# Attention logits in 32x64 tiles of TensorE: two column tiles of 64 keys for each head in place of one of 128

## The chip, the cores and the metric

The kernel runs on one core of a Trainium2 chip. The metric is the device time of one execution in microseconds (us); the median of three executions stands for the kernel.

## What is computed

The input x has the shape 4 x 128 x 64 x 64 (images, channels, rows, columns). Layer 0 normalises over the channels, adds a 3x3 depthwise convolution, and computes neighbourhood attention inside windows of 16x16 pixels: 2 branches, 4 heads of 32 channels, every pixel looks at the 5x5 pixels around it. Layer 1 treats the 4096 pixels of an image as tokens: causal linear attention, then a normalised recurrence over the tokens. The part that the change touches is this, for each window, branch b and head h:

```
k_nb = _patches(k, KSZ)
v_nb = _patches(v, KSZ)
scale = HD ** (-0.5)
logits = jnp.einsum('nbhdij,nbhdkij->nbhkij', q, k_nb) * scale
attn = jax.nn.softmax(logits, axis=3)
o = jnp.einsum('nbhkij,nbhdkij->nbhdij', attn, v_nb)
```

Here n is the window, d runs over the 32 channels of a head, k over the 25 neighbours and ij over the 256 pixels.

## The kernel before

**Staging.** The image is cut into 16 bands (4 images x 4 bands of 16 rows), each band into 4 windows of 16x16 pixels: 64 windows in all. For every band the kernel normalises and convolves (`norm_rows`, `convolve`, the taps on VectorE are L288), and for every window it goes through three steps that overlap between windows. `window_inputs` (L330) makes q, k (L337 on TensorE, evicted at L345) and v (L350, L357). `logits` (L370) makes the masked logits of both branches and their exponentials. `weighted` (L394) makes the denominators (L400), the weighted values (L412), and sends the denominators through DMA to be inverted on VectorE (L423 to L427) and spread again (L429, L431). `scaled` (L440, GpSimd) multiplies both. `layer1` (L608) is the linear attention of a band, written as a fixed order of steps; it runs two bands' halves in the gaps of later windows: among its lines are the output projection L465, transposes L212 by way of `turned`, queries and keys L494 (with L496 on ScalarE, L498 and L499 on VectorE), values L511 and L519, key transposes L529, scores L537 and L539, states L554 and L562, outputs L573, L575 and L587, and the product L602 with L603 and L604. After the last window comes a recurrence (L822, L835) and the output.

**The logits.** For a window, the four heads lie on partitions 0-31, 32-63, 64-95 and 96-127 of q and k, which are [128, 512]: branch times 256 pixels. Keys are handled in blocks of 8 rows of 16 pixels, so 128 keys; queries come in three pieces for each branch, rows 0 to 5, 6 to 9 and 10 to 15 (96, 64 and 96 pixels), each with the block of keys that holds all their neighbours: `BLOCKS`. Head h has a PSUM bank of its own, `sps[h]`: 128 keys on the partitions, 512 queries along the bank. First comes the mask (L377): a product of bfloat16 one-hot keys with query rows of 0 and -1e30, over all 512 queries. The six pieces are then accumulated onto it in float32 (L382), and four exponentials read the banks (L391). The stationary operand is the block of keys, [32 rows x 128 columns], the moving operand the queries, [32 x 96 or 64]. Four heads therefore use four row tiles of 32x128 in the array. A float32 matmul call appears in the trace as two weight loads and two matmuls, a bfloat16 call as one of each: per window 4 + 48 matmuls for the logits. The weighted values (L412) are the mirror image: the stationary operand is [128 keys x 32 channels], in four column tiles of 128x32, the moving operand has the same 96, 64 and 96 queries.

**The order of the work.** [...] `in_order` (L160) fixes that order for TensorE, VectorE, ScalarE and GpSimd. In the loop at L699, turn i issues `logits` of window i, `scaled` of window i-2, `weighted` of window i-1 and `window_inputs` of window i+1. Between these, six calls of `between` each take one step of `layer1` (`behind`) and one of normalisation and convolution (`ahead`). A window is called by its place wj = 0 to 3 in the band below; the layer-1 work of a band starts in the window with wj = 1 of the next band. All PSUM tiles of this part come from one pool of eight banks, used in rotation (L176), so the four banks of the logits must be free before the masks start.

## Time and profile before

| what | value |
|---|---|
| median of three executions | 929.56 us (928.55 to 930.22) |
| span of the profiled execution | 933.3 us |
| the 64 windows: first and last start of L382 | 26.2 and 803.8 us |
| TensorE matmuls busy | 878.8 us, 94% of the span |
| TensorE weight loads busy | 657.1 us, 70% |
| VectorE busy | 734.2 us, 79% |
| ScalarE busy | 539.5 us, 58% |
| GpSimd busy | 257.5 us, 28% |
| mean granted TensorE clock | 0.977 of full speed |

The page gives no other time for the profiled execution than its span, which is 3.7 us longer than the median. The timeline lists instructions in order of time, neighbours of one kind merged: start, duration, engine, line, operation, operands, and in brackets the idle time of the engine just before and who ended it. PE is the matmul side of TensorE, PEld its weight loads, DVE is VectorE, ACT ScalarE, POOL GpSimd. A matmul's recorded duration holds its latency too, so matmuls overlap, and a PE that shows no idle time may still stand for a fraction of a microsecond. In the steady state, 110 to 760 us, a band of four windows takes about 50.5 us; the four windows from L377 at 402.37 us on, for example, start at 402.37 (wj = 3), 413.57 (wj = 0), 427.82 (wj = 1) and 441.23 (wj = 2).

### The profile page before, as it was taken

To read this page: it belongs to the slowest core of one execution; us is meant where nothing else is said; L and a number is where in the kernel's file an instruction comes from. 1 tells how busy PE (TensorE), PEld (TensorE's weight loads), DVE (VectorE), ACT (ScalarE), POOL (GpSimd) and SP (SyncE) were. 2 spreads that over 40 slices of the span, in tenths; PEclk is the share of its full clock that TensorE was granted. 3 is DMA by queue.
4 is the path that set the end of the run, shared out by engine and by line. 5 is a ranking of instruction groups with operands and counts; after the bars stand their busy time and mean duration, and the time that the engine had idled before them with its cause. 6 is when DMAs were issued, how large, how long until landed. Compare 5 with 4: busy or idle time off the path is not lost.

```text
span 933.3 us, 26460 instructions
## 1 busy us (share of the span) xinstructions
PE 878.8 (94%) x10508; PEld 657.1 (70%) x10508; DVE 734.2 (79%) x2408; ACT 539.5 (58%) x1010; POOL 257.5 (28%) x358
## 2 busy tenths in 40 slices
PE   4968999999999999999999999999999999977894
PEld 3846787777787777778777777777777778755452
DVE  6454888889797879798888889787878787577694
ACT  3654656575656565665657575656666565522553
POOL 2112141323222232314132323323231403131174
PEclk9988999999999999999999999999999999989898
DMA  4111112122212121211212121212121111111853
GB/s 121 25 46 57 42 51 58 56 59 63 59 48 61 48 66 49 73 38 57 55 54 60 59 60 48 62 51 65 48 71 37 60 36 56 36 35 32 351 223 143
DMA packets 53045, 63.46 MB, mean 68 GB/s; under 512 B 22960, under 2 KB 33840, under 8 KB 52400
## 3 DMA queue, kind: packets, MB, share of 16 engines
q1 hardware_dynamic: 51184, 56.91, 19.6%
q10 hardware_dynamic: 1728, 4.77, 1.3%
q8 instruction: 85, 1.39, 0.7%
q14 instruction: 48, 0.39, 0.1%
HBM read 35.44 MB, written 17.30 MB: 57 GB/s over the span
## 4 chain that ended last, share of the span: by engine, by line
PE 59%; DVE 25%; DMA 5%; ACT 3%; issue 3%; POOL 3%; ACTq 0%; SPq 0%; DVEq 0%; POOLq 0%
DVE y L288 9%; PE bank L337 9%; PE bank L465 7%; PE bank L382 6%; PE bank L212 6%; PE bank L494 5%; PE bank L400 4%; PE bank L350 4%; PE bank L412 3%; PE bank L602 3%; DMA res<-resd 2%; DVE st L191 2%; PE bank L537 2%; DVE state L562 2%; DVE x L587 2%
## 5 line engine op out<-in xcount | busy, mean ns | idle before, releaser
L288 DVE SCALAR_TENSOR_TENSOR y<-ypad,cpe_w,y 128x512 f32<-128x512 f32 x240 | 191.5, 798 | 17.4 <-ACT y L286 13.9
L391 ACT ACTIVATE es<-bank 128x512 f32<-128x512 f32 x256 | 132.2, 603 | 77.3 <-PE bank L382 77.3
L440 POOL TENSOR_TENSOR oT<-o_sb,rden 128x512 f32<-128x512 f32 x64 | 83.9, 1311 | 247.3 <-DMA rden<-rd 221.5
L195 POOL TENSOR_SCALAR rs<-mv 128x4 f32<-128x4 f32 (+2 forms) x100 | 25.0, 250 | 366.1 <-DVE mv L193 162.8
L203 DVE TENSOR_SCALAR xn<-x,mv,rs 128x128 f32<-128x128 f32 x256 | 89.5, 411 | 26.5 <-POOL rs L196 26.5
L196 POOL TENSOR_TENSOR rs<-rs,mhalf 128x4 f32<-128x4 f32 (+2 forms) x100 | 106.3, 1063 | 8.3
L382 PEld LDWEIGHTS bank<-q,k 32*128 32x128 f32 x3072 | 97.8, 189 | 9.7 <-ACT k L345 8.5
L382 PE MATMUL bank<-q,k 32*128 32x96 f32 (+1 forms) x3072 | 96.3, 271 | 1.1 <-ACT k L345 1.1
L412 PEld LDWEIGHTS bank<-es,v_sb 128*32 128x32 f32 x3072 | 56.5, 110 | 30.0 <-issue 19.6
L465 PE MATMUL bank<-woT,oT 128*128 128x128 f32 x512 | 67.1, 287 | 6.8 <-POOL oT L440 6.8
L465 PEld LDWEIGHTS bank<-woT,oT 128*128 128x128 f32 x512 | 63.8, 200 | 10.8 <-POOL oT L440 8.5
L494 PE MATMUL bank<-xl,awT 128*128 128x512 f32 x128 | 70.0, 630 | 0.0
L412 PE MATMUL bank<-es,v_sb 128*32 128x96 f32 (+1 forms) x3072 | 69.7, 239 | 0.0
L337 PE MATMUL bank<-y2w,wqT 128*128 128x256 f32 x256 | 68.2, 390 | 1.0 <-DVE y2w L288 1.0
L357 ACT COPY v_sb<-bank 128x512 f32<-128x512 f32 x64 | 37.5, 586 | 54.7 <-PE bank L350 48.0
L400 PE MATMUL bank<-es,ones 128*32 128x512 f32 x512 | 68.9, 611 | 0.0
L337 PE MATMUL bank<-y2w,wkT 128*128 128x256 f32 x256 | 66.9, 385 | 0.0
L350 PE MATMUL bank<-wvT,y2w 128*128 128x256 f32 x256 | 66.4, 382 | 0.0
L345 ACT COPY q<-bank 128x512 f32<-128x512 f32 x64 | 37.6, 587 | 43.3 <-PE bank L337 41.2
L345 ACT COPY k<-bank 128x512 f32<-128x512 f32 x64 | 37.3, 583 | 37.6 <-PE bank L337 37.6
L191 DVE BATCH_NORM_STATS2 st<-x 128x6 f32<-128x128 f32 x256 | 55.5, 280 | 1.1
L337 PEld LDWEIGHTS bank<-y2w,wqT 128*128 128x128 f32 x256 | 46.7, 198 | 13.0 <-issue 7.2
(118 smaller groups left out, 1719.7 us busy)
## 6 DMA issues: line engine op xcount, KB each, us to landing
rden<-rd SPq DMA_DIRECT2D x64, 256.0 KB
v_sb<-v_sb SPq DMA_DIRECT2D x128, 64.0 KB
resd<-rs_o SPq DMA_DIRECT2D x32, 256.0 KB
out<-ot SPq DMA_DIRECT2D x32, 256.0 KB
xin<-in_xt SPq DMA_DIRECT2D x15, 512.0 KB
res<-resd SPq DMA_DIRECT2D x2, 2048.0 KB
res<-resd ACTq DMA_DIRECT2D x2, 2048.0 KB
dc<-den SPq DMA_DIRECT2D x64, 8.0 KB
```

Of the source, the lines that this page charges most:

```text
L196: nc.gpsimd.tensor_tensor(rs[:, :n], rs[:, :n], mhalf[:, :n], ALU.pow)
L203: nc.vector.tensor_scalar(xn[:, j, :], piece, mv[:, j, 0:1], rs[:, j : j + 1], ALU.subtract, ALU.mult)
L288: nc.vector.scalar_tensor_tensor(y2, src, cpe_w[:, tap : tap + 1], y2, ALU.mult, ALU.add)
L337: nc.tensor.matmul(pps[:, br * WT : (br + 1) * WT], wT[:, br * P : (br + 1) * P], y2, start=True, stop=True,)
L350: nc.tensor.matmul(vps[:, e * 256 : (e + 1) * 256], y2[:, e * P : (e + 1) * P], wvT, start=True, stop=True,)
L382: nc.tensor.matmul(sps[h][:, cols], w["k"][rows, k0 : k0 + P], w["q"][rows, cols], start=False, stop=(br, n) == pieces[-1],)
L391: nc.scalar.activation(es, sps[h], AF.Exp, scale=scale)
L400: nc.tensor.matmul(dps[rows], ones[:, :HD], w["es", h], start=True, stop=True)
L412: nc.tensor.matmul(ops[rows, cols], w["v"][:, n, c0 : c0 + HD], w["es", h][:, cols], start=(br, n) == pieces[0], stop=(br, n) == pieces[-1],)
L440: nc.gpsimd.tensor_tensor(oTs[n][:, :, :, wj * WS : (wj + 1) * WS], w["o"].rearrange("p (a r c) -> p a r c", a=BR, c=WS), w["rden"].rearra ...
L465: nc.tensor.matmul(yps[:, j * P : (j + 1) * P], oT[:, br, t], woT[:, br, :], start=br == 0, stop=br == BR - 1,)
L494: nc.tensor.matmul(zps, awT[:, m * P : (m + 1) * P], h.xl, start=True, stop=True)
```

## The change

The 128 keys of a block are multiplied as two stationary operands of 64 columns each. They are written to partitions 0-63 and 64-127 of the same bank. For each head this makes two column tiles of the array, 32x64, and for the four heads eight tiles. The mask is cut in the same way. The moving operands, the banks, the exponentials and everything that follows are unchanged; on every engine the instructions come in the same order as before. TensorE gets four more mask matmuls and 24 more float32 calls in each window.

```diff
+KC = 64
...
         for h in range(HEADS):
             rows = slice(h * HD, (h + 1) * HD)
 
-            nc.tensor.matmul(sps[h], mask_k[rows], mask_q[rows], start=True, stop=False)
+            for c in range(0, P, KC):
+                nc.tensor.matmul(
+                    sps[h][c : c + KC],
+                    mask_k[rows, c : c + KC],
+                    mask_q[rows],
+                    start=True,
+                    stop=False,
+                )
         for br, n in pieces:
             cols, k0 = spans(br, n)
             for h in range(HEADS):
                 rows = slice(h * HD, (h + 1) * HD)
-                nc.tensor.matmul(
-                    sps[h][:, cols],
-                    w["k"][rows, k0 : k0 + P],
-                    w["q"][rows, cols],
-                    start=False,
-                    stop=(br, n) == pieces[-1],
-                )
+                for c in range(0, P, KC):
+                    nc.tensor.matmul(
+                        sps[h][c : c + KC, cols],
+                        w["k"][rows, k0 + c : k0 + c + KC],
+                        w["q"][rows, cols],
+                        start=False,
+                        stop=(br, n) == pieces[-1],
+                    )
```

## The prediction

> **What bounds the kernel now.** I read the page first, its busy shares and its chain of waits.

> ```profile
> PE 878.8 (94%) x10508; PEld 657.1 (70%) x10508; DVE 734.2 (79%) x2408; ACT 539.5 (58%) x1010; POOL 257.5 (28%) x358
> ...
> PE 59%; DVE 25%; DMA 5%; ACT 3%; issue 3%; POOL 3%; ACTq 0%; SPq 0%; DVEq 0%; POOLq 0%
> ```

> TensorE looks like the bound, but a quarter of the chain lies on VectorE. So I took the chain in order of time over one band. First the windows starting at 402 (wj = 3) and 413 (wj = 0):

> ```profile
> 395.77 1.98 DVE xn L203 x4
> 397.75 0.66 DVE y L288
> ...
> 405.50 0.67 DVE y L288
> ...
> 406.72 0.58 ACT den L403
> 407.30 0.65 ACT low L496
> ...
> 420.58 0.36 DVE x L587
> ...
> 420.99 0.59 PE bank L212 x2
> ```

> From 395 to 421 us the chain never passes through a logits matmul. VectorE works without a break, except about 1.2 us at 407, where it waits for ScalarE (L403, L496), which had waited for VectorE's last tap. At 421 TensorE waits for VectorE. Then the windows starting at 428 (wj = 1) and 441 (wj = 2):

> ```profile
> 428.22 1.31 PE bank L382 x48
> ...
> 441.62 1.36 PE bank L382 x48
> 442.98 1.07 ACT es L391 x3
> ...
> 445.03 0.49 ACT wx L603
> ...
> 445.54 0.69 DVE stats L604
> ```

> Here both logits stages are on the chain, and the second, through the exponentials, releases VectorE (L604), which starts the next VectorE stretch. So a faster L382 pays in two windows of four.

> What a stage is made of shows in the timeline at 402 us, weight loads (PEld) beside matmuls (PE):

> ```profile
> 402.37 0.10 PEld L377 LDWEIGHTS <-mask_k 32*128 32x128 bf16 x4 [0.76 <-issue]
> 402.37 0.40 PE L377 MATMUL bank<-mask_q,mask_k 32*128 32x512 bf16 x4
> ...
> 402.38 1.53 PEld L382 LDWEIGHTS bank<-q,k 32*128 32x128 f32 x48
> ...
> 402.60 1.48 PE L382 MATMUL bank<-q,k 32*128 32x96 f32 x48
> ...
> 407.14 0.88 PEld L412 LDWEIGHTS bank<-es,v_sb 128*32 128x32 f32 x48 [0.76 <-DVE aT L539]
> 407.15 1.09 PE L412 MATMUL bank<-es,v_sb 128*32 128x96 f32 x48
> ```

> L382 and L412 have the same 48 matmuls with the same moving columns, four at a time in 12 rounds. Taking off the last matmul's duration (270 ns at L382, 249 ns at L412), the first-to-last start is 1.48 - 0.27 = 1.21 us with 128 stationary columns and 1.09 - 0.25 = 0.84 us with 32. L382 is slower because it waits for loads: its second round starts at 402.60, its last at 402.38 + 1.53 - 0.19 = 403.72, so one round of loads takes (403.72 - 402.60) / 10 = 112 ns.

> [...] 64 columns occur nowhere in the trace. [...] four tiles of L382 run side by side, and after its last matmul (start 403.81) L537 starts 0.19 us later. [...]

> **The change, part by part.**

> *Loads.* A round of 64-column loads should take 112 x 64/128 = 56 ns if all eight tiles load side by side. The trace shows it for four row tiles (L382) and four column tiles (L412: 48 loads in 0.88 us, each 110 ns), not for both at once. Bounds: 56 ns, or 112 ns if the two column tiles of a head take turns. I take 56. At L412's pace a 96-column round takes about 82 ns and a 64-column one about 56, so loads no longer lead and the stage runs at 0.84 us. Saved: 1.21 - 0.84 = 0.37 us per window.

> *More instructions.* 24 more float32 calls are 48 more loads and 48 more matmuls, but they sit in other tiles and run beside the old ones. Added is the stagger: pairs start about 7 ns apart in L412's rounds, so tiles five to eight end some 30 ns later; and four more mask pairs, about 10 ns. Bounds: 0 and 100 ns; I take 40. Net 0.33 us per window.

> *Mask.* 512 columns still stream once, 0.23 us from first mask to first L382 matmul (402.37 to 402.60); cost only the 10 ns above. [...]

> *Queues, other engines.* No wait, DMA or instruction of another engine is added or moved; the order on each engine is the same.

> *Where it pays.* wj = 2: wholly, 0.33. There are 14 such windows between 88 and 743 us: 4.6 us. wj = 1: after L382 come the transposes of `keep` (L212 at 429.46 to 429.95), the last of which needs L587, done at 429.46 on unbroken VectorE time; the next group could then start at about 429.63, so 0.32 of room, I take 0.30. In three of 13 bands (as at 383.42) TensorE already waits at L465 for GpSimd's L440; there nothing comes through. 10 x 0.30 = 3.0 us. wj = 3 and 0 up to 743 us: nothing; TensorE arrives earlier and waits longer at 421 us. Exception: the window at 99 us, still on the chain, 0.3. Startup: the first three windows (26, 35, 42 us) lie on the chain, 1.0; the next three are behind DMA and VectorE. Last band: from 729 to 815 us the chain is TensorE alone, so the five windows from 754 us on count, 1.6. The recurrence after 815 us is untouched. Sum: 4.6 + 3.0 + 0.3 + 1.0 + 1.6 = 10.5 us.

> The sum is made against the profiled span of 933.3 us, giving 922.8; nothing lies around that span which the change touches. The span is 3.7 us above the median of 929.56, so I take the saving from the median: 919.

> **Rivals.**

> *VectorE is not rigid* (12%). Then all 64 windows pay 0.33 us, 21 us: 908.5. For it: TensorE shows hardly any idle time. Against: at 421 us it demonstrably waits, and the chain there has no PE piece for 25 us.

> *The column tiles take turns* (10%). Two loads of 56 ns per head and round are 112 ns, as now; only the 40 ns are left, on the 14 + 10 + 1 + 3 + 5 = 33 windows on the chain counted above: +1.3, 931, within the bound of no change. Against: L412's four column tiles share all their rows, and their loads overlap (110 ns each, rounds of 56 to 82 ns).

> *TensorE cannot be fed* (15%; slower). The stage has 104 load-and-matmul pairs instead of 52, in hardly more than half the time: 0.23 + 0.84 = 1.07 us, or 10 ns per pair. The fastest long run in the trace is 17.5 ns per pair (L412), and that was bound by its columns, so the limit of the feed is unknown: between below 10 and 17.5 ns. At 17.5 the stage takes 104 x 17.5 = 1.82 us instead of 1.44, +0.38 per window. In wj = 3 and 0 about 0.5 us of waiting at 421 us and 0.4 at 426 us (an L212 group of 1.01 us against 0.60 elsewhere) cover it, so the 33 windows on the chain pay: +12.5, 942. It decides from 1.44 / 104 = 13.8 ns per pair on; between 10 and 13.8 the gain shrinks to nothing. [...] A variant at 12 ns gives about 925 (5%).

> *The change doesn't do what it says*: no; the order of instructions shows eight products per piece with 64 output partitions.

> **Numbers.** Likeliest (58%): 919, own range 914 to 924. Rivals 12% at 908.5, 5% at 925, 10% at 931, 15% at 942. Range 907 to 931: it leaves out the fed-limit case and little else. Within 0.2% (928 to 931.4) is what a measurement cannot tell from no change. Faster 0.75, same 0.10, slower 0.15.

> **What the profile after would show.** Right: L382's successor line with 96 matmuls in about 1.1 us instead of 1.48, loads of about 130 ns, the next group 1.3 us after the first mask instead of 1.64; the same 2.07 us of exponentials; the wait at L212 for VectorE in wj = 0 longer by about 0.6 us; windows wj = 1 and 2 shorter by 0.3 us each. Column tiles taking turns: loads of one head 56 ns apart in 12 rounds of 112. Feed limit: pairs evenly spaced at 12 ns or more, regardless of 96 or 64 columns. VectorE not rigid: windows wj = 3 and 0 shorter as well, no longer wait at 421. What would make me wrong is above all the VectorE stretch: its 1.2 us gap[...] may shift by more than what I count here.

## The result and the profile after

The changed kernel takes 926.39 us (median of 14 runs, 922.78 to 929.98), the kernel before in the same series 929.55 us (14 runs, 926.64 to 931.01). The ratio is 0.9973 with a 95% interval from 0.9958 to 0.9988: 3.2 us faster by the medians, 2.5 us by the ratio, 1.1 to 3.9 us by its interval. Forecast were 919 us, 10.5 us faster.

The profiled execution of the changed kernel has a span of 922.0 us and a time of 923.71 us, at a granted clock of 0.98. Its span seems to hit the 922.8 us that the prediction gave for the span. That is chance. The profiled execution of before was itself a long one: it starts its first logits at 26.2 us against 23.4 us here, and after its last window has started it runs 130.8 us against 127.7 us, although nothing was changed in either place. Between window 8 and window 60, where only the logits differ, the start-to-start distance fell from 654.7 to 651.4 us. These 3.3 us agree with the medians.

Line numbers have moved in the changed kernel: the mask is L379 (before L377), the logits L391 (L382), the weighted values L421 (L412), the transposes L213 (L212), the taps L289 (L288). First its page, the busy line and the chain of waits by engine:

```profile
PE 871.1 (94%) x13836; PEld 647.3 (70%) x13836; DVE 737.1 (80%) x2408; ACT 539.9 (59%) x1010; POOL 256.4 (28%) x358
...
PE 59%; DVE 26%; DMA 4%; ACT 4%; issue 3%; POOL 2%; ACTq 0%; DVEq 0%; SPq 0%; POOLq 0%
```

3328 more matmuls and as many more loads (13836 against 10508), and yet the busy shares and the chain are what they were. The chain in order of time, over one band from wj = 3 to wj = 2:

```profile
389.07 1.99 DVE xn L204 x4
...
400.03 0.58 ACT den L412
400.60 0.69 ACT low L505
...
414.10 0.36 DVE x L596
...
414.50 0.59 PE bank L213 x2
...
421.40 0.35 PE bank L379 x8
421.75 1.21 PE bank L391 x69
...
434.73 0.35 PE bank L379 x8
435.08 1.25 PE bank L391 x71
```

This is the picture of before: VectorE alone from 388 us to the transposes at 414.5 us, with the one gap at ScalarE (400 us), then logits on the chain in the two windows that start at 421 and 434 us. What failed can be seen in the pieces of L391: they are 1.21 and 1.25 us, against 1.31 and 1.36 us of L382. The timeline at 396 us shows one stage whole:

```profile
395.80 0.12 PEld L379 LDWEIGHTS <-mask_k 32*64 32x64 bf16 x8 [0.76 <-issue]
395.80 0.42 PE L379 MATMUL bank<-mask_q,mask_k 32*64 32x512 bf16 x8
395.82 1.41 PEld L391 LDWEIGHTS bank<-q,k 32*64 32x64 f32 x96
396.04 1.39 PE L391 MATMUL bank<-q,k 32*64 32x96 f32 x96
...
397.35 0.38 PE L546 MATMUL bank<-f,f 128*128 128x128 f32 x1
```

The 96 logits matmuls take 1.39 us where about 1.1 was forecast. Less the last one's duration (247 ns in the page's group of L391) they take 1.14 us from first to last start. The next group begins 1.55 us after the first mask, not 1.3. Over all windows after 110 us the medians of the single records are:

| stage of one window, ns | before | after | forecast |
|---|---|---|---|
| first mask to first logits matmul | 226 | 240 | 226 |
| first to last logits matmul | 1210 | 1147 | 840 |
| last logits matmul to next group | 200 | 171 | 240 |
| first mask to next group | 1636 | 1559 | 1306 |

(The forecast's extra 40 ns stand in the third row here.) A window gains 77 ns instead of 330. (Each row is a median of its own, so the rows do not add up to the last to the nanosecond.)

### The profile page after: what moved, and what is told of

Its sections match the earlier page's. It is cut to its first block, busy times and chain, and to the rows that moved or that the text cites. A ratio compares the mean times of both kernels' runs of the same rounds, so it can differ in the third digit from the quotient of the medians.

```text
span 922.0 us, 33116 instructions
## 1 busy us (share of the span) xinstructions
PE 871.1 (94%) x13836; PEld 647.3 (70%) x13836; DVE 737.1 (80%) x2408; ACT 539.9 (59%) x1010; POOL 256.4 (28%) x358
## 3 DMA queue, kind: packets, MB, share of 16 engines
q8 instruction: 111, 1.82, 0.8%
## 4 chain that ended last, share of the span: by engine, by line
PE 59%; DVE 26%; DMA 4%; ACT 4%; issue 3%; POOL 2%; ACTq 0%; DVEq 0%; SPq 0%; POOLq 0%
DVE y L289 9%; PE bank L338 8%; PE bank L474 7%; PE bank L213 6%; PE bank L391 6%; PE bank L503 5%; PE bank L409 4%; PE bank L351 4%; PE bank L421 3%; PE bank L611 3%; DMA res<-resd 2%; DVE st L192 2%; PE bank L546 2%; PE z L831 2%; DVE state L571 2%
## 5 line engine op out<-in xcount | busy, mean ns | idle before, releaser
L289 DVE SCALAR_TENSOR_TENSOR y<-ypad,cpe_w,y 128x512 f32<-128x512 f32 x240 | 190.1, 792 | 14.5 <-ACT y L287 11.0
L204 DVE TENSOR_SCALAR xn<-x,mv,rs 128x128 f32<-128x128 f32 x256 | 92.5, 422 | 26.6 <-POOL rs L197 26.6
L391 PEld LDWEIGHTS bank<-q,k 32*64 32x64 f32 x6144 | 89.1, 132 | 4.4 <-ACT k L346 1.8
L391 PE MATMUL bank<-q,k 32*64 32x96 f32 (+1 forms) x6144 | 90.7, 247 | 1.0 <-ACT k L346 1.0
L421 PEld LDWEIGHTS bank<-es,v_sb 128*32 128x32 f32 x3072 | 56.5, 110 | 30.7 <-issue 19.5
L421 PE MATMUL bank<-es,v_sb 128*32 128x96 f32 (+1 forms) x3072 | 69.9, 239 | 0.5 <-issue 0.5
```

The source lines that it names most:

```text
L204: nc.vector.tensor_scalar(xn[:, j, :], piece, mv[:, j, 0:1], rs[:, j : j + 1], ALU.subtract, ALU.mult)
L289: nc.vector.scalar_tensor_tensor(y2, src, cpe_w[:, tap : tap + 1], y2, ALU.mult, ALU.add)
L391: nc.tensor.matmul(sps[h][c : c + KC, cols], w["k"][rows, k0 + c : k0 + c + KC], w["q"][rows, cols], start=False, stop=(br, n) == pieces[-1],)
L421: nc.tensor.matmul(ops[rows, cols], w["v"][:, n, c0 : c0 + HD], w["es", h][:, cols], start=(br, n) == pieces[0], stop=(br, n) == pieces[-1],)
```

## The experiments

All ratios are against the kernel before, run on the same chip in the same series. "First to last" is the median from the first to the last start of a window's logits matmuls; "columns" are those that one tile multiplies for one branch.

| kernel | calls | columns | first to last, us | median, us | ratio (95% interval) |
|---|---|---|---|---|---|
| before | 24 | 256 | 1.210 | | 1 |
| after | 48 | 256 | 1.147 | 926.39 | 0.9973 (0.9958 to 0.9988) |
| joined | 32 | 224 | 0.848 | 920.13 | 0.9914 (0.9887 to 0.9942) |
| joined_wide | 32 | 256 | 0.888 | 922.11 | 0.9928 (0.9897 to 0.9958) |
| half_cols | 48 | 128 | 0.965 | 922.14 | 0.9936 (0.9921 to 0.9950) |
| few_cols | 48 | 48 | 0.910 | 919.79 | 0.9936 (0.9915 to 0.9957) |
| even_pieces | 48 | 240 | 1.083 | 926.30 | 0.9965 (0.9950 to 0.9980) |
| short_first | 48 | 256 | 1.098 | 925.29 | 0.9952 (0.9933 to 0.9972) |
| long_first | 48 | 256 | 1.120 | 927.01 | 0.9976 (0.9957 to 0.9994) |
| c_outer | 48 | 256 | 1.145 | 927.66 | 0.9987 (0.9972 to 1.0003) |
| kc32 | 96 | 256 | 3.69 | 1124.55 | 1.2123 (1.2081 to 1.2165) |

### Calls or columns

In the single records of the changed kernel the first eight matmuls start 3 to 4 ns apart, and the eight loads that follow them too: the column tiles do not take turns. Later the starts come 16 to 17 ns apart, one or two at a time (a float32 call holds two matmuls, so two at a time is one call every 16 to 17 ns). That suggested the feed theory: a float32 call (two loads and two matmuls) reaches TensorE no sooner than 16 to 17 ns after the one before it. Its rival: eight tiles stream their columns more slowly than four did, so that the stage goes with the columns. Four kernels were run first; the fourth, one_branch, stands under "Where a shorter stage pays".

**joined**: the four blocks of 4 key rows of a branch are multiplied once each, with all queries that need them, so the middle block's two halves are shared. The mask and the copies of v follow the new places of the keys.

```diff
+JOINED = ((0, 0, 0, 6), (64, 4, 2, 10), (0, 8, 6, 14), (64, 12, 10, 16))
...
+        for br in range(BR):
+            for pair in (JOINED[:2], JOINED[2:]):
+                for h in range(HEADS):
+                    rows = slice(h * HD, (h + 1) * HD)
+                    for c, key, r0, r1 in pair:
+                        cols = slice(br * WT + r0 * WS, br * WT + r1 * WS)
+                        k0 = br * WT + key * WS
...
```

> Edit: the column tiles are kept, but each block of 64 keys is multiplied once with all the queries that need it (96 or 128 of them) in place of once per piece, so a window has 32 float32 calls in place of 48, and 448 moving columns per tile in place of 512. The middle block's keys change places, in the mask and in v. Theory F (TensorE is fed one float32 call about every 16.6 ns once what is queued is used up; the 48 calls of the changed kernel are more than the feed carries): 32 calls are 0.53 us of feed, below the columns (about 0.76 us), so the stage from the first mask matmul to the next group falls from 1.56 us to about 1.2 us, and the time by 12 to 16 us against the kernel before, 914 to 918. Theory S (the two column tiles of a head share a path for their moving columns, so the stage follows the columns): 1.15 x 448/512 = 1.0 us, stage 1.4 us, time about 920 to 922.

Measured: 920.13 us, and the next group 1.26 us after the first mask. The stage fits the feed theory; the time alone would not have decided, for it lies above what that theory gave and at the edge of what the other gave. With all of 33 windows paying 0.38 us it would have been 12.4 us faster, and it is 7.6 (5.4 to 10.5 by the interval). Where the rest went stays open: between window 8 and window 60 the profiled execution is 8.7 us shorter than that of before (646.0 against 654.7 us), which is 0.38 us for each of the 23 windows counted there.

**half_cols**: the changed kernel, each call over the first half of its queries; the other half keeps the mask alone.

```diff
             cols, k0 = spans(br, n)
+            cols = slice(cols.start, (cols.start + cols.stop) // 2)
```

> Edit: the changed kernel with the same calls, each with only the first half of its queries (48 or 32 moving columns); half of the logits are left out, the mask alone stands there. Theory F (feed): the number of calls is unchanged, so the stage falls only to the feed, 48 x 16.6 = 0.8 us after the masks, about 1.2 us from first mask to next group; calls come evenly every 16 to 17 ns. Theory S (columns): the part after the masks halves from 1.15 to 0.57 us, stage 0.98 us.

Measured: half of the columns save 0.18 of 1.147 us. First mask to next group is 1.35 us, above the feed theory's 1.2 and far above 0.98. Columns are not what sets most of the stage, but they are not free either.

**kc32**: 32 keys a call, 16 tiles of 32x32, 96 calls a window (`KC = 32`).

> Edit: KC = 32, four column tiles of 32 keys for each head, 16 tiles, 96 float32 calls and 16 mask calls per window. Theory F (feed of about 16.6 ns per call): 96 x 16.6 = 1.6 us and the masks, the stage becomes about 2.0 us against 1.56 us in the changed kernel and 1.64 us before; slower than before by 0.35 us in the windows on the chain, +10 to +20 us, 940 to 950. Theory S (moving columns share a path by column tile): four tiles share it, the stage doubles to about 2.5 us or more, over 955. If neither holds and only the columns of one tile count (0.84 us): stage 1.25 us, 917.

Measured: 1124.55 us, far above the 940 to 950 us of the feed theory; the column theory had said only "over 955". This kernel met something else besides. Its timeline at 432 us:

```profile
432.25 0.43 PE L379 MATMUL bank<-mask_q,mask_k 32*32 32x512 bf16 x16
432.30 1.91 PEld L391 LDWEIGHTS bank<-q,k 32*32 32x32 f32 x146
432.48 1.88 PE L391 MATMUL bank<-q,k 32*32 32x96 f32 x145
435.93 0.76 PE L391 MATMUL bank<-q,k 32*32 32x64 f32 x47 [1.57 <-issue]
```

145 of 192 matmuls run, then TensorE stands still for 1.57 us, and no engine is named as the cause ("issue"). In its list of waits (microseconds in total, times, longest) this is by far the first line:

```profile
PE bank L391 <- issue: 76.2, 38, 4.2
```

The DMA table of the page has a queue that carries instructions (packets, megabytes, share). After, and then kc32:

```profile
q8 instruction: 111, 1.82, 0.8%
```

```profile
q8 instruction: 163, 2.67, 1.0%
```

A packet is 1.82 MB / 111 = 16.4 KB. The change added 26 packets to the 85 of before, and 6656 records (33116 against 26460): 256 records for each packet. In kc32, of the 36 standstills of over 0.6 us inside L391, every one has such a packet landing in it or at most 0.9 us before it, and the stream resumes 1.20 to 1.60 us after the landing (median 1.41). That they go together is shown; that TensorE stands because it waits for the packet is inferred from it. In 16 of the 64 windows no such packet is under way during the stage, and none of these has a standstill. The changed kernel has none inside L391 in any window, and its stage takes 1.147 us in the median both in the 19 windows during which a packet is under way and in the 45 others. So these packets are not what holds the changed kernel back. The standstills are 76 of the 197 us that kc32 loses, and not all of the rest is taken apart here; its granted clock was 0.93.

The 16 undisturbed windows take 2.23 us from first to last logits matmul (the 3.69 of the table hold standstills) and 2.62 us from first mask to next group. That is what the column theory gave (2.5 us or more), not the 2.0 of the feed theory: kc32 doubles the calls, but also the column tiles of a head, so it can't tell the two apart, and calls at 16.6 ns each were too cheap an estimate for it. While the stream of the timeline above flows, its pace is (1.88 - 0.24) / 144 = 11.4 ns per matmul, close to the 1147 / 95 = 12.1 ns of the changed kernel, with loads half as wide and twice as many tiles. The width of the loads does not set that pace.

Two more runs do separate calls from columns.

**few_cols**: only the first 16 queries of each call (the other queries keep the mask alone).

```diff
             cols, k0 = spans(br, n)
+            cols = slice(cols.start, cols.start + WS)
```

> The changed kernel with the same 48 logits calls per window, each multiplying only its first 16 queries instead of 96 or 64 (the logits of the other queries are left out, they keep the mask alone). Feed theory: the number of instructions is the same, so the calls still come 16 to 17 ns apart once the queue is used up; first mask to last logits matmul start stays at 1.2 to 1.35 us (halving the queries took it from 1.56 to 1.35), the time is 919 to 923. Column theory (the queries still set the pace): half the queries gave 1.35, so a sixth gives about 0.9 or less, and the time is 915 or less.

**joined_wide**: the joined version with 128 queries in each of its pieces, so the columns of the changed kernel in two thirds of its calls.

```diff
-JOINED = ((0, 0, 0, 6), (64, 4, 2, 10), (0, 8, 6, 14), (64, 12, 10, 16))
+JOINED = ((0, 0, 0, 8), (64, 4, 2, 10), (0, 8, 6, 14), (64, 12, 8, 16))
```

> The joined version with four pieces of 128 queries for each branch (rows 0-7, 2-9, 6-13, 8-15), so 32 calls a window stream as many columns through every tile as the 48 calls of the changed kernel do: 256 for each branch. Feed theory (the number of calls limits the changed kernel): the stage is far shorter than the changed kernel's 1.147 us from first to last logits matmul, near the 0.84 us that the same columns take in the weighted values, 0.85 to 0.98; the time is 919 to 923. Column theory (the gain of the joined version came from its fewer columns, 224 instead of 256): the stage comes back to 1.1 or more, and the time to 925 or more.

The timeline of few_cols at 431 us, then of joined_wide at 406 us:

```profile
431.17 0.42 PE L379 MATMUL bank<-mask_q,mask_k 32*64 32x512 bf16 x8
...
431.41 1.11 PE L392 MATMUL bank<-q,k 32*64 32x16 f32 x96
```

```profile
405.63 0.42 PE L380 MATMUL bank<-mask_q,mask_k 32*64 32x512 bf16 x8
...
405.87 1.16 PE L394 MATMUL bank<-q,k 32*64 32x128 f32 x64
```

With 16 columns instead of 96 or 64, the 96 matmuls still take 0.910 us. From the first mask to the last start it is 1.15 us, just below the 1.2 that the feed theory gave and well above the 0.9 of the other. The first 16 matmuls, whose first eight loads were done during the mask, take 87 ns, or 5.4 ns each; the other 80 take 823 ns, or 10.3 ns each, and in the evenest part (64th to 88th start) 202 / 24 = 8.4 ns, a call every 16.8 ns. The loads can't explain that: while they lie ready, they start into one tile at 2, 58 and 117 ns after the first matmul, so eight tiles would get through 12 rounds in about 0.63 us (an estimate: 28 ns to the second round, ten more at 58 ns, 23 ns within the last), not 0.910. So eight tiles are served nearly as fast as hoped at first, and more slowly after some 20 matmuls. That the first instructions lay ready in TensorE and the later ones had to arrive is a reading that fits both paces, 5.4 and 10.3 ns; it is inferred, and what sets the pace of arrival these runs do not show.

In joined_wide the same columns as in the changed kernel take 0.888 us, near the 0.84 us of L412. Both kernels thus lie by the feed theory and far from the other. Yet the changed kernel takes 1.147 us, 0.24 us more than its calls need with few columns, and 0.26 us more than its columns need with few calls.

### Why both limits together cost more

Three orders of the same work were tried, and one kernel with pieces of equal length. **c_outer** puts four heads' first column tiles ahead of the four second ones:

```diff
-            for h in range(HEADS):
-                rows = slice(h * HD, (h + 1) * HD)
-                for c in range(0, P, KC):
+            for c in range(0, P, KC):
+                for h in range(HEADS):
+                    rows = slice(h * HD, (h + 1) * HD)
```

> The changed kernel with the column tiles in the outer loop of each piece: four heads with keys 0-63, then four heads with keys 64-127, instead of the two column tiles of a head next to each other. Feed theory: the number of calls is the same, and so is the stage, 1.10 to 1.20 us from first to last logits matmul, and the time, 924 to 929. Theory that the order of the tiles holds calls up behind busy tiles: the stage moves by more than 0.1 us one way or the other, and the time by more than 3 us.

**long_first** and **short_first** change the order of the pieces, and **even_pieces** makes them equal (row 15 keeps the mask alone). Their lines, in this order:

```diff
+    order = [p for p in pieces if p[1] != 1] + [p for p in pieces if p[1] == 1]
...
+    order = [p for p in pieces if p[1] == 1] + [p for p in pieces if p[1] != 1]
...
+            cols = slice(br * WT + 5 * n * WS, br * WT + 5 * (n + 1) * WS)
```

> The changed kernel with the order of its six pieces changed: the four of 96 queries first, the two of 64 last. A round of 16 pairs in eight tiles needs 165 ns for 96 columns by its columns, 112 ns for 64, and 133 to 135 ns by its calls (eight at 16.7 ns). Theory of the alternation (the loss of 0.25 us over either limit alone comes from a short piece that uses the queue up and long pieces that wait behind it): the four long rounds run at 165 ns each from a queue that the feed refills, the short ones at 112 to 135, 0.90 to 1.00 us from first to last logits matmul instead of 1.147. Theory that feed and columns add up whatever the order: 1.10 to 1.20 us.

> The reverse: the two pieces of 64 queries first, then the four of 96. Theory of the alternation: the short rounds use up the queue at 112 to 135 ns each, then one late round and four near 165 ns: 0.95 to 1.05 us from first to last. Theory that feed and columns add up whatever the order: 1.10 to 1.20 us.

> The changed kernel with six pieces of 80 queries (rows 0-4, 5-9 and 10-14; the logits of row 15 are left out, it keeps the mask alone), 240 columns in place of 256 for each branch. A round of 16 pairs needs 137 ns by its columns and 133 by its calls. Theory of the alternation: no piece waits behind another, 0.85 to 0.95 us from first to last. Theory that feed and columns add up: 1.05 to 1.15 us, in proportion between 0.965 us at 128 columns and 1.147 at 256.

Measured, first to last: 1.145, 1.120, 1.098 and 1.083 us. The first two and the last lie where the theory that supply and columns add up put them; short_first is 2 ns below its bound and 48 ns above the other theory's. The theory that long and short pieces in turn make the loss falls. What makes the two add up none of these runs isolates. It stays open why the changed kernel takes 1.15 us and not, say, 1.0.

### Where a shorter stage pays

The prediction held that VectorE takes back what wj = 3 gains. **one_branch** is the kernel before with the logits of the second branch left out (mask alone), which shortens the stage by 0.67 us:

```diff
-        for br, n in pieces:
+        for br, n in pieces[:3]:
...
-                    stop=(br, n) == pieces[-1],
+                    stop=(br, n) == pieces[2],
```

> Edit: the kernel before, with the logits of the second branch left out (three pieces in place of six; the mask alone stands there). It makes the stage shorter without any column tile: 24 of 48 matmuls, 6 of 12 rounds of 112 ns, so 0.6 to 0.67 us less per window. It asks how much of a shorter stage reaches the end. If VectorE's stretch through the windows wj = 3 and wj = 0 is rigid: these two together stay as long as before, only about 33 windows pay, -20 us, 909. If it is not: all 64 pay, -38 us, 891.

Measured: 913.27 us, ratio 0.9845 (0.9811 to 0.9879), 14.5 us faster; 22 windows' worth of 0.67 us, where a stage that pays everywhere would give 64. It is 5.5 us less than the 20 us that a rigid VectorE stretch gave, and far from the 38 of the other forecast. Most of what is missing is a ceiling of wj = 1, read from the table below. To take the cover away, three kernels leave out taps 6 to 8 of the depthwise convolution on VectorE:

```diff
-            else:
+            elif tap < 6:
```

> The kernel before with taps 6 to 8 of the depthwise convolution left out (a third of the nine taps of every window on VectorE), so VectorE has about 2 us less to do in each window. Used as the base of the next two runs. Theory R (the VectorE stretch of wj = 3 and wj = 0 is what ate the stage's saving): the waits of TensorE at the layer-1 transposes for VectorE disappear, TensorE then sets all 64 windows; the time falls by about the half microsecond of waiting at these places in 13 to 16 bands, to 905 to 922. Theory N (VectorE is not what eats it): the time falls too, but the differences of the next two runs from this one stay at 3 and 8 us.

> The changed kernel with taps 6 to 8 left out, to be compared with the kernel before with the same taps left out. The stage saves 0.08 us per window in the changed kernel. Theory R: with VectorE relieved all 64 windows pass it on, 64 x 0.08 = 5 us below that run. Theory N: 3 us below it as with all taps. The difference of 2 us is at the edge of what can be told; the next run is the sharper one.

> The joined version (32 calls per window, 32x64 tiles) with taps 6 to 8 left out, to be compared with the kernel before with the same taps left out. Its stage saves 0.38 us per window. Theory R: 64 x 0.38 = 24 us below that run, 18 to 25. Theory N: about 8 us below it, as with all taps.

Measured: 912.62, 908.60 and 889.90 us, ratios 0.9845 (0.9827 to 0.9863), 0.9807 (0.9784 to 0.9830) and 0.9618 (0.9596 to 0.9639). The three taps are 96 of VectorE's 256, and leaving them out took its busy time from 734 to 676 us: 0.9 us a window, not the 2 us said beforehand. With VectorE relieved, joined is 22.7 us below its base, as 64 x 0.38 = 24 us foretold; with all taps it was 7.6 us. The changed kernel is 4.0 us below, which tells 5 from 3 no better than was said beforehand. The starts of windows show the place. Mean distance to the next window in microseconds, by place, over 13 bands (windows 8 to 59), in one profiled execution of each:

| kernel | wj = 3 | wj = 0 | wj = 1 | wj = 2 |
|---|---|---|---|---|
| before | 11.20 | 14.09 | 13.46 | 11.60 |
| after | 11.12 | 14.05 | 13.40 | 11.53 |
| joined | 10.82 | 14.39 | 13.25 | 11.22 |
| one_branch | 10.53 | 14.84 | 13.25 | 10.93 |
| six_taps_before | 11.20 | 13.00 | 13.40 | 11.60 |
| six_taps_joined | 10.82 | 12.64 | 13.10 | 11.22 |

In joined, wj = 3 gains 0.38 us and wj = 0 gives 0.30 back; in one_branch 0.67 and 0.75. With six taps wj = 0 gains 0.36 us of its own instead. wj = 1 gains 0.21 in both joined and one_branch, though the second saves nearly twice as much: a ceiling. Three of its 13 windows stay at 13.8 us in both, the other ten gain 0.27 us. The giving back can be read in the lists of waits, of before and then of joined:

```profile
PE bank L212 <- DVE x L587: 3.7, 11, 0.6
```

```profile
PE bank L214 <- DVE x L599: 10.8, 14, 1.0
```

and in that of six_taps_joined, where this line has left the top of the list (one wait of 0.6 us remains):

```profile
PE bank L214 <- DVE xf L205: 11.4, 3, 8.2
PE bank L477 <- POOL oT L452: 6.3, 5, 3.0
PE bank L214 <- DVE xn L205: 6.0, 5, 2.5
```

L599 and L214 are the former L587 and L212: TensorE waits for VectorE's last layer-1 tile 14 times, 10.8 us in all, against 3.7 us in 11 waits before.

### One part of the change alone

**mask_only** has only the mask in 32x64 tiles, **logits_only** only the logits; each takes the other of the two calls from the kernel before (edits against the changed kernel).

```diff
-                for c in range(0, P, KC):
-                    nc.tensor.matmul(
-                        sps[h][c : c + KC, cols],
...
+                nc.tensor.matmul(
+                    sps[h][:, cols],
...
-            for c in range(0, P, KC):
-                nc.tensor.matmul(
-                    sps[h][c : c + KC],
...
+            nc.tensor.matmul(sps[h], mask_k[rows], mask_q[rows], start=True, stop=False)
```

> One part of the change alone: the mask in eight 32x64 tiles, the logits as before in four 32x128 tiles. If a change of tiling makes TensorE finish what runs before it goes on, the first logits matmul starts 0.1 to 0.2 us later than the 0.24 us after the first mask, the stage grows from 1.44 us to 1.55 to 1.65, and the time is 2 to 6 us above the kernel before: 929 to 936. If it costs nothing: the stage stays at 1.44 us and the time at that of the kernel before.

> The other part alone: the logits in eight 32x64 tiles, the mask as before in four 32x128 tiles. With a drain between the two, 0.1 to 0.2 us: stage 1.5 to 1.6 us instead of 1.39 in the changed kernel, the gain is gone, the time within 4 us of the kernel before, 926 to 933. Without: stage 1.37, the time that of the changed kernel, 923 to 927.

Measured: 939.67 us, ratio 1.0129 (1.0090 to 1.0168), and 932.16 us, ratio 1.0026 (1.0010 to 1.0042). Timeline of mask_only, then of logits_only:

```profile
402.73 0.42 PE L379 MATMUL bank<-mask_q,mask_k 32*64 32x512 bf16 x8
403.08 1.43 PEld L390 LDWEIGHTS bank<-q,k 32*128 32x128 f32 x48 [0.23 <-issue]
403.08 1.59 PE L390 MATMUL bank<-q,k 32*128 32x96 f32 x48
```

```profile
400.25 0.40 PE L378 MATMUL bank<-mask_q,mask_k 32*128 32x512 bf16 x4
400.57 1.25 PEld L384 LDWEIGHTS bank<-q,k 32*64 32x64 f32 x96 [0.23 <-issue]
400.57 1.44 PE L384 MATMUL bank<-q,k 32*64 32x96 f32 x96
```

In both, the first load of the logits starts together with their first matmul, 0.32 to 0.35 us after the first mask; with the mask and the logits in tiles of one shape (timeline of after, above) it starts 20 ns after the mask's first load. So with a change of tile shape between the two, the first load came about 0.3 us later; that it waits until the masks are finished fits these times, but was not shown, as the recorded ends of matmuls are modelled. It costs twice: the first logits matmul comes 0.11 us (mask_only) or 0.09 us (logits_only) later than in the changed kernel, and the stream that follows, with no loads done ahead, takes 1.323 instead of 1.210 us and 1.196 instead of 1.147 us. mask_only thus loses 0.24 us a window, more than the 0.1 to 0.2 expected, and 9.9 us in all, beyond the 2 to 6 expected; 33 windows give 7.9. In logits_only the next group comes 0.055 us later than before, 1.8 us over 33 windows, and 2.4 us are measured. So the mask had to be cut together with the logits, as the change does: there the first logits matmul comes 240 ns after the first mask, 14 ns later than before.

## Why the prediction was right or wrong

**Loads side by side: right.** The page has 132 ns a load, as forecast, and loads of all eight tiles start 3 to 4 ns apart. In few_cols, where columns hold nothing up, the next load into a tile follows after 56 to 59 ns (2, 58 and 117 ns); 56 was forecast, and 112 if the column tiles took turns. That rival is out.

**The stage at L412's pace: wrong, and this is the step that failed.** The prediction wrote: "so loads no longer lead and the stage runs at 0.84 us. Saved: 1.21 - 0.84 = 0.37 us per window." Loads no longer lead, that much is true. But the next limit was taken to be the columns alone, and it is the number of calls together with the columns: 1.147 us. Why the two together cost more than either (0.910 and 0.888 us) stays open. Of 0.37 us per window, 0.063 came. The first 16 matmuls of the stage do run at L412's pace (165 ns for them in the changed kernel, where 82 ns per eight were forecast); most of the other 80 do not.

**More instructions at 40 ns: wrong in the same way.** The words "they sit in other tiles and run beside the old ones" count tiles, not what feeds them. With few columns the 96 pairs need 0.910 us by themselves; this alone is above the 0.84 that the prediction gave for everything. The mask was rightly priced: first mask to first logits matmul grew by 14 ns.

**The rival "cannot be fed": its mechanism is the one that came, at a milder size.** It counted pairs over the whole stage, 10 ns needed and 13.8 ns the point from which the change loses. Measured by that count are (240 + 1147) / 104 = 13.3 ns, just inside the band in which "the gain shrinks to nothing". The variant at 925 us was given 5% and is the nearest case. Its sign in the profile, evenly spaced pairs "regardless of 96 or 64 columns", came only in part, since columns still count. What had spoken for a faster feed was one stage at 17.5 ns per pair that its columns bound: it bounded the feed from one side only, and the likeliest case took the other end.

**Where it pays: right where the saving is large; the change itself can't tell.** With 0.077 us in place of 0.33, the 33 windows of the prediction give 2.5 us, all 64 would give 4.9; measured are 3.2 (1.1 to 3.9). Between window 8 and window 60 the count gives 1.8 us, all windows 4.0, and the two profiled executions differ by 3.3. VectorE taking back the gain of wj = 3 is not seen at 0.08 us: wj = 0 did not grow, and TensorE's wait for the last layer-1 tile was 2.5 us in 5 waits, not longer than the 3.7 of before. But joined and one_branch show it at 0.3 to 0.7 us, and the six-tap kernels show it gone. The rival "VectorE is not rigid" is out: joined would have gained 24 us with all taps, not 7.6. The ceiling of wj = 1 exists too: 0.30 us in 10 of 13 bands were predicted, and joined and one_branch gain 0.27 in ten of 13.

**A version that beats both:** joined, 920.13 us, ratio 0.9914 (0.9887 to 0.9942) to before. It has the tiles of the change with 32 calls in place of 48, and reaches 0.848 us from first to last, which the prediction had expected of 48.

## What to carry to other kernels

Smaller tiles trade columns of weight load for a larger number of instructions (here 132 ns a load in place of 189, and 96 matmuls a window in place of 48): before cutting a stage, divide its new time by the new number of calls, and take no pace as given that the trace does not show for a long run of calls in many tiles. Cut so that the count doesn't rise, by larger moving operands or shared stationary ones (32 calls took 0.848 us in joined and 0.888 us in joined_wide, 48 calls 1.147 us), and change neighbouring stages of one bank together: with the mask alone or the logits alone in the smaller tiles, the kernel was 9.9 and 2.4 us slower than before. And ask of each window who waits next: here about half of the windows could not pass on what their stage saved until VectorE had less to do.
